# Attention 1: v's blocks filled by transfers in place of copies, operand transfers on two queues

## The chip, the core and the metric

The kernel runs on one core of a Trainium2 chip. The metric is the device time of one execution in microseconds (us), a median over runs. The engines are PE (matrix products; its weight loads are the profile's PEld), DVE (vector), ACT (activations), POOL (GpSimd) and SP, which here only issues transfers (DMAs). Each engine works through its own queue in order and waits for the others by semaphores. DMAs can be issued from SP, POOL or ACT; a DMA that has to wait keeps everything behind it on the issuing queue waiting.

## What is computed

Two layers over x (8 sequences of 1024 tokens, 256 wide): an attention with its residual and normalisation, and a block of a second attention and a mixture of experts. The change concerns only the first attention, in which **every token attends within itself**: its q, k and v are 16 heads of 64 numbers each, and the 64x64 scores are made inside one head of one token.

```python
Q = (x @ Wq + bq).reshape(b, s, H, C) * inv_sqrt_c      # H, C = 16, 64
K = (x @ Wk + bk).reshape(b, s, H, C)
V = (x @ Wv + bv).reshape(b, s, H, C)
scores = jnp.einsum('bshq,bshk->bshqk', Q, K)            # an outer product per token and head
scores = jnp.where(triu_mask, -jnp.inf, scores)
w = jax.nn.softmax(scores, axis=-1)
attn = jnp.einsum('bshqk,bshk->bshq', w, V)
x = layernorm(x + attn.reshape(b, s, H * C) @ Wo + bo)
```

## The kernel before

`phase_a` does this layer; phases B and C do the rest and are not touched. It works through 64 tiles of 128 tokens. A tile `t` is cut into 8 chunks `c`, each of them 64 tokens (`ww = c // 4`, the half of the tile) by four heads (`c % 4`). The main loop writes out by hand, chunk by chunk, what each engine is given; since every engine keeps its order, the order of these calls is the schedule.

**Scores as block matrices.** For PE, an outer product per token and head becomes a matrix product with block-diagonal operands: `R` holds q (and row maxima) on the diagonal blocks, `L` holds k. There are two buffers of each. `build(t, r)` (line 360) fills one pair for the chunks 2r and 2r+1 with 24 DMAs: 8 for `R` (line 370, 16 rows of 2 KB each, issued from POOL) and 16 for `L` (line 376, 64 pieces of 128 B each, issued from SP). A DMA into a buffer waits until the scores of two chunks earlier have read it. `gather(r)` (line 384) puts a small memset, the *event*, on POOL; it waits for all 24 DMAs, and the score matmuls (`scores`, line 418) wait for it alone. ACT takes the exponentials (line 433).

**Sums.** `sums` (lines 453 and 463) multiplies the exponentials with v on PE. Its weights are columns of `V`, one buffer for each half `ww`: 128 partitions, for each head and each of four token groups `u` a block of 32 columns (four tokens times 8, with v in columns 0 to 3 of a token's 8 and a one in column 4, which sums the weights themselves). Four of these matmuls of 32 columns run side by side on quarters of the PE array. The quotients are laid by tokens again: ACT evicts to `S` (line 479), and POOL issues 32 DMAs a tile `nd<-S` (line 489).

**How V is filled.** `proj_v` (line 291) makes v transposed, two halves of 512 columns in PSUM, and DVE evicts each with the bias to `vT` as (channel, chunk of channels, token) at line 306. `spread_v` (line 313) then copies it on DVE into the blocks of V: 8 copies for each half of the tile and each half of the channels, 32 a tile (line 320; 32 partitions, 96 or 128 values each). The calls stand in `fill_a` and `fill_b` at chunks 0 and 6.

**One PSUM buffer `ps`** serves the projections of k, q and v for the next tile, two halves each, at chunks 0 to 5 (`between`), and the output projection at 6 and 7. A projection cannot start before DVE has evicted the one before it; q's evictions are line 331.

**Side work on DVE and POOL.** The rest of the tables `head`, `fill_a`, `middle` and `fill_b` says at which chunk which side job is issued: `divide` (lines 573 to 580: the sums are added up, the reciprocal taken and multiplied) for the tile before, `extrema` (running maxima and minima of k, two scans of DVE), `products` (two multiplications on POOL) and `maxima` (one on DVE) for the next tile, `token_scores`, `token_less`, `token_exp`, `token_sums` for four heads of the present tile that are done without PE, `normal` (line 629) for the normalisation and `store` for the finished rows. An entry's sign says for which tile: "+" the next, "" this, "-" the one before, "--" two before.

**Buffers that matter.** `vT`, `r`, `lo`, `att` have one buffer each, k, qm, x1o and xr two, the pair of score banks three.

Of the kernel before, what the change touches and what calls it, by code (L numbers as in the profile page):

```python
# [165 lines left out]
def phase_a(tc, a, ident, x1_d, norm_scalars, share, view):  # L166
# [19 lines left out]
    with (  # L186
# [68 lines left out]
        for i in range(2):  # L255
            Ls.append(wp.tile([P, 16, 4, 32], FP, name=f"L{i}"))
            R = wp.tile([P, 4, 8, C1], FP, name=f"R{i}") if i else share["R"]
            nc.gpsimd.memset(R, 0.0)
            Rs.append(R)
            V = wp.tile([P, NV, 4, 32], FP, name=f"V{i}") if i else share["V"].rearrange("p j h u c -> p (j h) u c")[:, :NV]  # L260
            nc.gpsimd.memset(V, 0.0)
            for aa in range(4):
                nc.gpsimd.memset(V[32 * aa : 32 * aa + 32, :, :, 8 * aa + 4 : 8 * aa + 5], 1.0)
            Vs.append(V)
# [26 lines left out]
        def proj_v(t, half):  # L291
            if half == 0:
                state["vT", t] = op.tile([P, HID // P, P], FP, name="vT")
            vT = state["vT", t]
            ps = pps.tile([P, 512], FP, name="ps")
            for i in range(4):
                ch = 4 * half + i
                for c in range(DC):
                    nc.tensor.matmul(  # L299
                        ps[:, i * P : (i + 1) * P],  # L300
                        w["v"][:, c, chunk[ch] * P : (chunk[ch] + 1) * P],
                        xT_of[t][:, c, :],
                        start=c == 0,
                        stop=c == DC - 1,
                    )
            nc.vector.tensor_tensor(
                vT[:, 4 * half : 4 * half + 4, :],
                ps.rearrange("p (i t) -> p i t", i=4),
                bv[:, 4 * half : 4 * half + 4, None].to_broadcast([P, 4, P]),
                ALU.add,  # L310
            )

        def spread_v(t, ww, half):

            src = state["vT", t].rearrange("p i (w u a b) -> p i w u a b", w=2, u=4, a=4)
            for qd in (2 * half, 2 * half + 1):
                at, n = (H1, (H1 - HT) // 2) if qd % 2 else (0, H1 // 2)
                V = Vs[ww][:, at : at + 2 * n].rearrange("p (i r) u (a b) -> p i r u a b", r=2, a=4)
                for aa in range(4):
                    nc.vector.tensor_copy(  # L320
                        V[32 * aa : 32 * aa + 32, :, qd // 2, :, aa, 0:4],
                        src[32 * qd : 32 * qd + 32, :n, ww, :, aa, :],
                    )
# [36 lines left out]
        def build(t, r):  # L360
# [7 lines left out]
            for b in range(4):  # L368
                for s in range(2):
                    moved.append((None, nc.gpsimd.dma_start(R[:, b, s, b, :], q[:, b, s, cols])))  # L370
# [65 lines left out]
        def sums(t, c, which):  # L436
# [7 lines left out]
            for x, h in enumerate(heads):  # L444
                hp = h0 + h
                v = 2 * slot[hp // 2] + hp % 2
# [46 lines left out]
        def token_v(t, ps):  # L493

            n = TC // P
            for i in range(n):
                nc.tensor.transpose(ps[:, (2 + i) * P : (3 + i) * P], state["vT", t][:, HID // P - n + i, :], ident)
# [230 lines left out]
        def lead_v(k):  # L728
# [91 lines left out]
        spread_v(0, 0, 0)  # L820
        spread_v(0, 0, 1)
# [9 lines left out]
        for t in range(NT + 1):  # L831
            live, more = t < NT, t + 1 < NT
            for c in range(8):
# [17 lines left out]
                if c == 4 and t > 1:  # L851
# [863 lines left out]
```

## Time and profile before

| | |
|---|---|
| median of 13 runs | 4911.7 us (4898.5 to 4935.2) |
| the profiled execution | 4906.4 us, span in the profile 4904.6 us |
| tiles of phase A | about 62 like ones, 64.5 us apart on the mean (stores at 212.7 to 4144.4 us) |
| busy shares | PE 91%, DVE 85%, ACT 73%, POOL 71% |
| mean granted PE clock | 0.96 |
| DVE copies into V (L320) | 2048, 631.0 us in all |
| DMAs on SP in phase A | L<-k 4088, 0.64 us each to issue |
| DMAs on POOL in phase A | R<-qm 2048 and nd<-S 2048, 0.49 us each |

The profile has one execution. A line such as "PE ps L330 <- DVE qm L331: 244.8, 62, 5.8" in the view of waits says that PE, about to run line 330, stood idle for 244.8 us in all, 62 times, at most 5.8 us, until DVE had done line 331. In the view of groups a line reads: source line, engine, operation, written tile <- read tiles, shapes, count | busy us, mean ns of one | idle before, by releaser. In the timeline a line reads: start us, length us, engine, line, operation, tiles, shapes, count, and in brackets the idle time before it with what ended it. An engine that is busy without a break is not always the bound: what counts is which wait ends last at the place where the time is lost.

### The profile page before, as it was taken

To read this page: it belongs to the slowest core of one execution; us is meant where nothing else is said; L and a number is where in the kernel's file an instruction comes from. 1 tells how busy PE (TensorE), PEld (TensorE's weight loads), DVE (VectorE), ACT (ScalarE), POOL (GpSimd) and SP (SyncE) were. 2 spreads that over 40 slices of the span, in tenths; PEclk is the share of its full clock that TensorE was granted. 3 is DMA by queue.
4 is the path that set the end of the run, shared out by engine and by line. 5 is a ranking of instruction groups with operands and counts; after the bars stand their busy time and mean duration, and the time that the engine had idled before them with its cause. 6 is when DMAs were issued, how large, how long until landed. Compare 5 with 4: busy or idle time off the path is not lost.

```text
span 4904.6 us, 169315 instructions
## 1 busy us (share of the span) xinstructions
PE 4462.2 (91%) x70232; PEld 2998.2 (61%) x70232; DVE 4164.9 (85%) x6686; ACT 3560.9 (73%) x5015; POOL 3471.7 (71%) x5672
## 2 busy tenths in 40 slices
PE   7999999999999999999999999999999999888785
PEld 4666666666666666666666666666666666555564
DVE  7888888888888988898888889888888897577778
ACT  5778777777787887778877877777887788344334
POOL 6777777777777777778777777877777776232346
PEclk9999999999999999999999999999999999999897
DMA  2222212222221222222212222221222222133443
GB/s 80 48 49 50 48 48 50 50 49 48 49 52 46 50 50 49 48 49 52 49 48 51 50 49 48 50 49 47 52 52 48 48 49 71 53 79 77 130 150 117
DMA packets 521271, 285.66 MB, mean 58 GB/s; under 512 B 373425, under 2 KB 439345, under 8 KB 520497
## 3 DMA queue, kind: packets, MB, share of 16 engines
q1 hardware_dynamic: 378466, 113.23, 11.9%
q0 software_dynamic: 139264, 159.69, 10.4%
q8 instruction: 550, 9.01, 0.8%
q10 hardware_dynamic: 2768, 1.91, 0.1%
q14 instruction: 223, 1.83, 0.1%
HBM read 72.84 MB, written 33.85 MB: 22 GB/s over the span
## 4 chain that ended last, share of the span: by engine, by line
PE 60%; DVE 27%; DMA 3%; POOL 3%; issue 2%; ACT 2%; SPq 2%; DVEq 0%; ACTq 0%; POOLq 0%
PE pair L418 16%; PE sum L453 11%; PE sum L463 7%; DVE att L579 5%; PE ps L299 5%; PE ps L618 5%; PE ps L330 4%; PE pair L407 4%; DVE V L320 4%; DVE nd L578 3%; DVE att L580 3%; PE ps L288 2%; SPq L376 2%; PE pair L589 1%; ACT s L1029 1%
## 5 line engine op out<-in xcount | busy, mean ns | idle before, releaser
L433 ACT ACTIVATE e<-pair 128x1024 f32<-128x1024 f32 x2560 | 2481.4, 1022 | 534.1 <-PE pair L418 503.5
L418 PE MATMUL pair<-R,L 32*128 32x128 f32 (+1 forms) x28672 | 1408.7, 321 | 4.8 <-POOL event L384 4.1
L489 POOL DMA_DIRECT2D nd<-S x2048 | 972.6, 483 | 610.6 <-ACT S L479 548.1
L418 PEld LDWEIGHTS pair<-R,L 32*128 32x128 f32 x28672 | 1103.5, 187 | 118.4 <-issue 64.9
L370 POOL DMA_DIRECT2D R<-qm x2048 | 989.6, 490 | 140.6 <-PE pair L418 118.1
L453 PE MATMUL sum<-e,V 128*32 128x256 f32 x12288 | 963.9, 385 | 4.1 <-ACT S L479 4.0
L463 PE MATMUL sum<-e,V 128*32 128x128 f32 x16384 | 792.5, 278 | 0.0
L479 ACT COPY S<-sum 128x512 f32<-128x512 f32 (+1 forms) x1024 | 552.3, 539 | 312.6 <-PE sum L463 312.6
L463 PEld LDWEIGHTS sum<-e,V 128*32 128x32 f32 x16384 | 503.1, 111 | 433.9 <-issue 114.9
L320 DVE COPY V<-vT 32x128 f32<-32x128 f32 (+1 forms) x2048 | 631.0, 308 | 29.3
L330 PE MATMUL ps<-wq,xT 128*128 128x512 f32 x512 | 332.4, 784 | 250.8 <-DVE qm L331 244.8
L544 POOL TENSOR_TENSOR s<-s,qm 128x1024 f32<-128x1024 f32 (+2 forms) x320 | 517.1, 1636 | 3.1
L579 DVE RECIPROCAL att<-nd 128x384 f32<-128x384 f32 (+1 forms) x192 | 438.1, 2282 | 3.9 <-DMA nd<-S 1.7
L407 PE MATMUL pair<-late,sel 32*128 32x256 bf16 (+1 forms) x5120 | 402.1, 299 | 4.2 <-ACT e L433 4.2
L453 PEld LDWEIGHTS sum<-e,V 128*32 128x32 f32 x12288 | 305.4, 109 | 151.4 <-issue 63.4
L76 POOL TENSOR_SCALAR ve<-mv 128x1 f32<-128x1 f32 x128 | 85.0, 664 | 435.1 <-DVE mv L74 417.1
L563 DVE TENSOR_TENSOR s<-s,vt 128x1024 f32<-128x1024 f32 (+2 forms) x320 | 382.0, 1194 | 11.1
L562 DVE TENSOR_REDUCE part<-s 128x64 f32<-128x1024 f32 (+3 forms) x320 | 300.8, 940 | 73.8 <-ACT s L548 73.8
L330 PEld LDWEIGHTS ps<-wq,xT 128*128 128x128 f32 x512 | 108.1, 234 | 384.9 <-DVE qm L331 269.7
L564 DVE TENSOR_REDUCE part<-s 128x64 f32<-128x1024 f32 (+3 forms) x320 | 305.0, 953 | 11.0
L536 DVE TENSOR_TENSOR s<-k,qm 128x1024 f32<-128x1024 f32 (+2 forms) x320 | 292.2, 946 | 0.0
L407 PEld LDWEIGHTS <-sel 32*128 32x128 bf16 x5120 | 135.2, 92 | 242.0 <-issue 234.4
(253 smaller groups left out, 6148.3 us busy)
## 6 DMA issues: line engine op xcount, KB each, us to landing
R<-qm POOLq DMA_DIRECT2D x2048, 32.0 KB, 2.1
nd<-S POOLq DMA_DIRECT2D x2048, 32.0 KB, 2.0
L<-k SPq DMA_DIRECT2D x4088, 8.0 KB
rows_d<-yx SPq DMA_DIRECT2D x32, 512.0 KB
xT<-in_xT SPq DMA_DIRECT2D x64, 128.0 KB
xr<-in_x SPq DMA_DIRECT2D x64, 128.0 KB
x_d<-x1o SPq DMA_DIRECT2D x64, 128.0 KB
w<-in_w SPq DMA_DIRECT2D x32, 256.0 KB
```

The costliest lines, as they stand in the source:

```text
L320: nc.vector.tensor_copy(V[32 * aa : 32 * aa + 32, :, qd // 2, :, aa, 0:4], src[32 * qd : 32 * qd + 32, :n, ww, :, aa, :],)
L330: nc.tensor.matmul(ps, xT_of[t][:, c, :], w["q"][:, c, cols], start=c == 0, stop=c == DC - 1)
L370: moved.append((None, nc.gpsimd.dma_start(R[:, b, s, b, :], q[:, b, s, cols])))
L407: nc.tensor.matmul(bank[u][:, at : at + width].rearrange("p (n i) -> p n i", i=n)[:, :, 0:32], sel[pr].rearrange("p a j -> p (a j)"), late ...
L418: one = nc.tensor.matmul(bank[u][:, x * 4 * n : (x + 1) * 4 * n].rearrange("p (b i) -> p b i", i=n), Lt[pr, 2 * (h0 + h) + jb].rearrange(" ...
L433: nc.scalar.activation(es[i], pair[i], AF.Exp)
L453: nc.tensor.matmul(dst[32 * u : 32 * u + 32], Vs[ww][:, v, u, :], e[u // 2][:, u % 2, x * 256 : (x + 1) * 256].rearrange("p (b i) -> p b i ...
L463: nc.tensor.matmul(dst[32 * u : 32 * u + 32], Vs[ww][:, v if alone else H1 + v, u, :], e2[u // 2][:, u % 2, h * P : (h + 1) * P].rearrange ...
L479: nc.scalar.copy(S[:, :, at : at + 2, i0:].rearrange("p b h i -> p h b i"), ps[:, : 8 * (C1 - i0)].rearrange("p (h b i) -> p h b i", h=2, ...
L489: nc.gpsimd.dma_start(tok[:, b, s, (h0 - G) * C1 : (h0 + G) * C1], Sx[:, 4 if s else b, b, :])
L544: nc.gpsimd.tensor_tensor(s, s, m, ALU.subtract)
L579: nc.vector.reciprocal(att[:, cols], nd[:, 1, cols])
```

## The change

Four things are changed together.

- **V is filled by DMA.** `V` is kept as four quarters (`blocks`, by halves of a channel chunk and of the kind of head), each laid out as 32 columns `m`, then channel chunks `i`, then token groups `u`. A block column's values for all `i` and `u` are thus neighbours (128 or 96 B), and `spread_v` is 16 DMAs from SP for each half of the tile, each 32 partitions by 4 such rows. So that the source has the same layout, `proj_v` reads x in the order (w, m, u) instead of token order, and the eviction writes `vT` as (m, i, u). The block for the four token-wise heads is evicted a second time in token order, `vo`, by two operations on DVE. `sums` reads its weights from the quarters, 32 columns in steps of n x 4 values (n is 8 or 6).
- **Operand transfers:** all of R is issued from SP; of the 16 DMAs for L the odd `u` go from POOL, the even from SP. In the first tile the L that ACT issued now go from POOL too.
- **Order:** the second `products` moves from chunk 5 to the head of chunk 7 (ahead of the event there), the second `extrema` from 4 to 5, the second `maxima` from 6 to 7, the last `divide` from 1 to 2, `normal` from the first half of chunk 2 to the end of chunk 4, `store` from 4 to 6. The two calls of `spread_v` for each half become one, at chunks 0 and 6 in `fill_a`.
- x1o has one buffer instead of two.

```diff
+            V = wp.tile([P, NV * P], FP, name=f"V{i}") if i else share["V"].rearrange("p j h u c -> p (j h u c)")[:, : NV * P]
             nc.gpsimd.memset(V, 0.0)
+            blocks, at = [], 0
+            for qd in range(4):
+                n = (H1 - HT * (qd % 2)) // 2
+                blocks.append(V[:, at : at + n * P].rearrange("p (m i u) -> p m i u", m=32, u=4))
+                at += n * P
+                for aa in range(4):
+                    nc.gpsimd.memset(blocks[qd][32 * aa : 32 * aa + 32, 8 * aa + 4 : 8 * aa + 5], 1.0)
+            Vs.append(blocks)
...
                     nc.tensor.matmul(
-                        ps[:, i * P : (i + 1) * P],
+                        ps[:, i * P : (i + 1) * P].rearrange("p (w m u) -> p w m u", w=2, u=4),
                         w["v"][:, c, chunk[ch] * P : (chunk[ch] + 1) * P],
-                        xT_of[t][:, c, :],
+                        xT_of[t][:, c, :].rearrange("p (w u m) -> p w m u", w=2, u=4),
...
             nc.vector.tensor_tensor(
-                vT[:, 4 * half : 4 * half + 4, :],
-                ps.rearrange("p (i t) -> p i t", i=4),
-                bv[:, 4 * half : 4 * half + 4, None].to_broadcast([P, 4, P]),
+                vT[:, :, 4 * half : 4 * half + 4, :].rearrange("p m i u -> p i m u"),
+                ps.rearrange("p (i m u) -> p i m u", i=4, u=4),
+                bv[:, 4 * half : 4 * half + 4, None, None].to_broadcast([P, 4, 32, 4]),
                 ALU.add,
             )
+            if half == 1:
+                for i in range(TC // P):
+                    nc.vector.tensor_scalar(
+                        state["vo", t][:, i, :].rearrange("p (w u m) -> p w u m", w=2, u=4),
+                        ps[:, (2 + i) * P : (3 + i) * P].rearrange("p (w m u) -> p w u m", w=2, u=4),
+                        bv[:, 6 + i : 7 + i], None, ALU.add,
+                    )
...
-        def spread_v(t, ww, half):
+        def spread_v(t, ww):
+            src = state["vT", t].rearrange("p (w a b) i u -> p w a b i u", w=2, a=4)
+            for qd in range(4):
+                V = Vs[ww][qd].rearrange("p (a b) i u -> p a b i u", a=4)
+                n = V.shape[3]
                 for aa in range(4):
-                    nc.vector.tensor_copy(
-                        V[32 * aa : 32 * aa + 32, :, qd // 2, :, aa, 0:4],
-                        src[32 * qd : 32 * qd + 32, :n, ww, :, aa, :],
+                    nc.sync.dma_start(
+                        V[32 * aa : 32 * aa + 32, aa, 0:4].rearrange("p b i u -> p b (i u)"),
+                        src[32 * qd : 32 * qd + 32, ww, aa, :, :n, :].rearrange("p b i u -> p b (i u)"),
                     )
...
-                    moved.append((None, nc.gpsimd.dma_start(R[:, b, s, b, :], q[:, b, s, cols])))
+                    moved.append((None, nc.sync.dma_start(R[:, b, s, b, :], q[:, b, s, cols])))
...
-                    queue = nc.scalar if t + r == 0 and aa % 2 else nc.sync
+                    queue = nc.gpsimd if u % 2 else nc.sync
...
-                            Vs[ww][:, v, u, :],
+                            v[0][:, :, i, u],
...
-                        Vs[ww][:, v if alone else H1 + v, u, :],
+                        v[0 if alone else 1][:, :, i, u],
...
-            o = xp.tile([P, D], FP, name="x1o")
+            o = op.tile([P, D], FP, name="x1o")
...
         head = {
...
+            7: [("+", products, 1)],
         fill_a = {
-            0: [("", spread_v, 1, 0)],
-            2: [("--", normal), ("-", residual)],
+            0: [("", spread_v, 1)],
+            2: [("-", residual)],
             3: [("+", products, 0)],
-            5: [("+", products, 1), ("-", residual_bias)],
-            6: [("+", spread_v, 0, 0)],
+            5: [("-", residual_bias)],
+            6: [("+", spread_v, 0)],
...
         fill_b = {
-            0: [("", spread_v, 1, 1), ("+", extrema, 0)],
-            1: [("-", divide, 1), ("", token_scores, "F"), ("-", divide, 2)],
-            2: [("", token_sums, "A")],
+            0: [("+", extrema, 0)],
+            1: [("-", divide, 1), ("", token_scores, "F")],
+            2: [("-", divide, 2), ("", token_sums, "A")],
             3: [("", token_sums, "B"), ("", token_scores, "C")],
-            4: [("+", maxima, 0), ("+", extrema, 1), ("", token_sums, "F"), ("-", turn)],
-            6: [("+", spread_v, 0, 1), ("+", maxima, 1)],
-            7: [("+", token_scores, "A"), ("+", token_scores, "B"), ("", divide, 0)],
+            4: [("+", maxima, 0), ("--", normal), ("", token_sums, "F"), ("-", turn)],
+            5: [("+", extrema, 1)],
+            7: [("+", maxima, 1), ("+", token_scores, "A"), ("+", token_scores, "B"), ("", divide, 0)],
...
-                if c == 4 and t > 1:
+                if c == 6 and t > 1:
                     store(t - 2)
```

More of the change, by code (lines that the diff above doesn't have):

```diff
@@ L259, in phase_a @@
             Rs.append(R)
-            V = wp.tile([P, NV, 4, 32], FP, name=f"V{i}") if i else share["V"].rearrange("p j h u c -> p (j h) u c")[:, :NV]
+            V = wp.tile([P, NV * P], FP, name=f"V{i}") if i else share["V"].rearrange("p j h u c -> p (j h u c)")[:, : NV * P]
             nc.gpsimd.memset(V, 0.0)
-            for aa in range(4):
-                nc.gpsimd.memset(V[32 * aa : 32 * aa + 32, :, :, 8 * aa + 4 : 8 * aa + 5], 1.0)
-            Vs.append(V)
+            blocks, at = [], 0
[6 more added lines that the diff above has]
+            Vs.append(blocks)
         def preset(i):
@@ L292, in proj_v @@
             if half == 0:
-                state["vT", t] = op.tile([P, HID // P, P], FP, name="vT")
+                state["vT", t] = op.tile([P, 32, HID // P, 4], FP, name="vT")
+                state["vo", t] = op.tile([P, TC // P, P], FP, name="vo")
             vT = state["vT", t]
@@ L306, in proj_v @@
             nc.vector.tensor_tensor(
-                vT[:, 4 * half : 4 * half + 4, :],
-                ps.rearrange("p (i t) -> p i t", i=4),
-                bv[:, 4 * half : 4 * half + 4, None].to_broadcast([P, 4, P]),
+                vT[:, :, 4 * half : 4 * half + 4, :].rearrange("p m i u -> p i m u"),
+                ps.rearrange("p (i m u) -> p i m u", i=4, u=4),
+                bv[:, 4 * half : 4 * half + 4, None, None].to_broadcast([P, 4, 32, 4]),
                 ALU.add,
             )
-        def spread_v(t, ww, half):
[L315 to L318, printed above, removed]
+            if half == 1:
[3 more added lines that the diff above has]
+                        ps[:, (2 + i) * P : (3 + i) * P].rearrange("p (w m u) -> p w u m", w=2, u=4),
+                        bv[:, 6 + i : 7 + i],
+                        None,
+                        ALU.add,
+                    )
[4 more added lines that the diff above has]
+                n = V.shape[3]
                 for aa in range(4):
-                    nc.vector.tensor_copy(
-                        V[32 * aa : 32 * aa + 32, :, qd // 2, :, aa, 0:4],
-                        src[32 * qd : 32 * qd + 32, :n, ww, :, aa, :],
+                    nc.sync.dma_start(
+                        V[32 * aa : 32 * aa + 32, aa, 0:4].rearrange("p b i u -> p b (i u)"),
+                        src[32 * qd : 32 * qd + 32, ww, aa, :, :n, :].rearrange("p b i u -> p b (i u)"),
                     )
@@ L445, in sums @@
                 hp = h0 + h
-                v = 2 * slot[hp // 2] + hp % 2
+                v = Vs[ww][2 * (hp % 2) : 2 * (hp % 2) + 2]
+                i = slot[hp // 2]
                 if alone:
@@ L496, in token_v @@
             for i in range(n):
-                nc.tensor.transpose(ps[:, (2 + i) * P : (3 + i) * P], state["vT", t][:, HID // P - n + i, :], ident)
+                nc.tensor.transpose(ps[:, (2 + i) * P : (3 + i) * P], state["vo", t][:, i, :], ident)
             state["vt", t] = xp.tile([P, TC], FP, name="vt")
@@ L819, in phase_a @@
         proj_v(0, 1)
-        spread_v(0, 0, 0)
-        spread_v(0, 0, 1)
+        spread_v(0, 0)
         token_v(0, pps.tile([P, 512], FP, name="ps"))
```

## The prediction

> **What bounds the kernel now.** I read the page's busy shares first, then the waits of PE, then single tiles in the timeline and in the windows view, and last the chain. A tile is 128 tokens; the stores of the finished rows (x_d<-x1o, one a tile) lie 64.5 us apart on the mean from 212.7 us to 4144.4 us, so about 62 such tiles make four fifths of the span and everything that the diff touches.
>
> ```profile
> PE 4462.2 (91%) x70232; PEld 2998.2 (61%) x70232; DVE 4164.9 (85%) x6686; ACT 3560.9 (73%) x5015; POOL 3471.7 (71%) x5672
> ```
> ```profile
> PE ps L330 <- DVE qm L331: 244.8, 62, 5.8
> ```
>
> PE is the busiest, and the only long wait of PE in a tile is one: the second half of the q projection (L330) waits until DVE has evicted the first half (L331), because both use the one PSUM buffer `ps`. It happens in every tile. The windows view of a common tile and of a rare one (60.5 us) shows what it costs; columns are length, busy time of PE, PEld, DVE, ACT, POOL, then the granted clock:
>
> ```profile
> 1511.60:1577.10 65.50, 60.44 (x1040) 39.73 (x1040) 56.77 (x83) 49.70 (x63) 48.71 (x83) 0.95 0.20 48
> 406.90:467.40 60.50, 59.05 (x1054) 39.91 (x1050) 52.06 (x86) 50.91 (x65) 48.49 (x83) 1.00 0.22 52
> ```
>
> The common tile has 5.06 us of idle PE and a clock of 0.95; the short one has 1.45 us and a full clock. So PE's own work is 59.05 us a tile, and the common tile pays twice: for the wait, and for slower matmuls after it. The timeline shows both, first on DVE, then on PE:
>
> ```profile
> 1533.75 6.66 DVE L320 COPY V<-vT 32x128 f32<-32x128 f32 x8
> ...
> 1549.93 2.54 DVE L579 RECIPROCAL att<-nd 128x384 f32<-128x384 f32 x1
> 1552.50 1.90 DVE L580 TENSOR_TENSOR att<-att,nd 128x384 f32<-128x384 f32 x1
> 1554.33 1.22 DVE L629 TENSOR_SCALAR x1o<-r,mv,rs 128x256 f32<-128x256 f32 x1
> 1555.47 0.68 DVE L331 SCALAR_TENSOR_TENSOR qm<-ps,bias 128x512 f32<-128x512 f32 x1
> ```
> ```profile
> 1544.84 1.99 PE L330 MATMUL ps<-wq,xT 128*128 128x512 f32 x4
> ...
> 1556.20 3.78 PE L330 MATMUL ps<-wq,xT 128*128 128x512 f32 x4 [5.06 <-DVE qm L331]
> ```
>
> The first projection ends at 1546.8, but DVE is solidly busy from 1532 and reaches its eviction only at 1555.5; after the wait the same four matmuls take 3.78 us for 1.99 (the windows view grants a clock of 0.50 there).
>
> **Part 1: what goes.** The copies of L320 go (32 a tile, 631.0 us in all, 9.9 us a tile). In the stretch before the eviction of q that is 1.8 + 6.66 us; the last division (2.54 + 1.90) and the normalisation x1o (1.22) move behind it, to chunks 2 and 4. DVE would reach L331 some 14 us earlier, where 1555.5 - 1546.8 = 8.7 us are enough. So the wait goes whole, and DVE falls from 56.8 to about 47 us a tile. Behind the next eviction of q stand the last division and the sums of A (4.4 + 3.7 us), a chunk is over 7 us: late by at most 1 us, and the next user of `ps` comes a chunk later. Gain 64.5 - 59.05 = **5.4 us a tile**, 338 us over 62; nothing in the trace speaks for more. It is covered by nothing else: PE is the chain there.
>
> **Part 2: PE reads in steps.** The v projection now reads x by tokens 16 columns (64 B) apart, and the sums load V weights in steps of 96 or 128 B. No matmul or weight load of this trace reads fp32 in such steps, so I bound it. Below: no cost, because the sums run four at a time, four streams side by side: eight L453 of 256 columns take 0.46 us, 0.23 for each round of four, where a single stream (L618, 256 columns, 1.73 us for 8) takes 0.22; the reading side isn't short. Above: the two nearest rows, reductions of DVE over 512 values, one with values 256 B apart, the other packed:
>
> ```profile
> L1388 DVE TENSOR_REDUCE loc<-run 128x64 f32<-128x512 f32 x1 | 1.0, 1012 | 0.0
> L1424 DVE TENSOR_REDUCE total<-run 128x64 f32<-128x512 f32 x1 | 0.7, 686 | 0.0
> ```
>
> The steps cost 326 ns over 512 values, 0.64 ns each. For the projection: 32 matmuls a tile of 128 columns, 82 ns each, now one every 0.111 us (2.05 us for 16): **+2.6 us a tile**, straight on PE. I take this end: it is the only row with the pattern. For the weights: 32 columns, 20 ns, behind a round of matmuls (0.108 us or more) except the first of the 16 groups: **+0.3 us**. If instead the four loads of a round share one way, 128 columns cost 82 ns in each of the 64 rounds of L463, whose matmuls leave no room: +5.2 us, the upper bound.
>
> This row can be weighed against a rule. The Trainium skill, page "Advanced Engine Details and Errata", section "Memory Cachelines", says that SBUF is read at full rate only where at least two accesses fall on one 16-byte line; here every value lies on a line of its own, so it speaks against this change. DVE's row agrees in kind (1.5 times), no run here shows PE. Taken as half rate for PE, an estimate from the page, the projection would cost 3.4 us a tile in place of 2.6 and the sum would be some 50 us higher.
>
> **Part 3: queues.** POOL gives its 32 transfers R to SP and takes 32 of the 64 L. An L has 64 pieces of 128 B where R has 16. What POOL takes for 64 is not in the trace; the nearest rows are 16 rows and, with an index, 128 rows:
>
> ```profile
> L370 POOL DMA_DIRECT2D R<-qm x2048 | 989.6, 490 | 140.6 <-PE pair L418 118.1 <-issue 10.0 <-DVE nd L578 5.1
> ...
> L1505 POOL DMA_INDIRECT g<-rows_d,token x64 | 61.6, 962 | 57.6 <-ACT w L1362 38.4 <-issue 18.0 <-PE ps L1519 1.2
> ```
>
> Between 0.49 and 0.96 us; a straight line by pieces gives 0.69, which I take: +0.2 x 32 = 6.4 us a tile, POOL 48.7 to 55 of 60. POOL matters through one instruction, the event that lets PE use the new operands (L384). Its tightest place is the chunk pair 0 and 1:
>
> ```profile
> 1528.08 3.89 POOL L370 DMA_DIRECT2D R<-qm  x8
> 1531.97 3.80 POOL L489 DMA_DIRECT2D nd<-S  x8
> 1535.79 3.83 POOL L544 TENSOR_TENSOR s<-s,qm 128x1024 f32<-128x1024 f32 x2
> 1539.56 0.09 POOL L384 MEMSET event<- 1x1 f32 x1
> ```
>
> PE asked for it at 1541.1, 1.5 us later. The eight L add 1.6 us, and the second products (3.3 us) now stand in chunk 7 ahead of the event and the root of the norm, where POOL idled 2.2 us: everything after starts 1.1 us later. 1.6 + 1.1 - 1.5 = **+1.2 us a tile** (0 at 0.49 us an L; 3.4 at 0.96). Waiting behind it are only the next L and nd. The page "DMA: Bandwidth & Descriptors" of the Trainium skill ("Anatomy of one DMA") holds that many descriptors are emitted before their cost shows; by that this term is 0.
>
> SP issued 64 L of 0.69 us (11.08 for 16) and now issues 32 L, 32 R, 32 V. R and V cost 0.34 to 0.64; the nearest is lg_d<-bias, 128 pieces, 0.43. In all 22 + 28 + 1.3 = 51 us of about 63. In chunks 6 and 0 the V come behind the operands: 8 x 0.43 + 8 x 0.69 = 9 us for operands (11 before), then 7 us for V, 16 of the 14 to 17 us that a pair of chunks lasts; V is first read 6.7 us into chunk 0 for one half and in chunk 4 for the other. I put it at 0, hidden under the scores; at 0.64 each the next operands start 4 us late and about 2 us reach PE. R behind the last maxima (now chunk 7) waits about as long as the event, already counted. DVE's two extra evictions `vo` (about 0.3 us each) and the eviction by blocks lie in DVE's new slack. The single buffer for x1o: its next write is a tile after the store, 0. The first tile pays once: R and V now queue on SP behind the last maxima, about +5 us.
>
> **Sum.** A tile: -5.4 + 2.6 + 0.3 + 1.2 = -1.3 us; x 62 = -81, + 5 = -76. The profiled execution took 4906.4 us (span 4904.6), the median of the runs is 4911.7, 0.1% above it; against the median: **4835 us**.
>
> **Rivals.**
> - *PE doesn't mind the steps.* For it: four streams at full rate. Against it: the DVE row. -5.4 + 1.2 = -4.2 a tile, 4655 us; with L at 0.49 as well 4580.
> - *Weight loads become the bound (slower).* Place: the 64 rounds of L463 a tile, whose loads (0.110 us) are already as long as their matmuls (0.108). Price +5.2 for +0.3: 3.6 us a tile, +225, 5140 us. It decides from 20 ns more a round (64 x 0.020 = 1.3). Against it: the loads of a round start 7 ns apart and end together.
> - *POOL becomes the bound.* At 0.96 us an L its busy time is 48.7 + 15 = 64 us, with its waits for ACT (1 to 3 us a tile) 66 to 67, above the 64.5 of today: +2 x 62, about 5040 us. For it: 64 pieces, not 16.
> - *The change doesn't do what it says:* PE still waits at L330. Only if DVE is held by another wait; then PE stalls as now and pays for the steps: about 5070.
>
> **Chances.** Forecast (4750 to 4915) 0.36; steps free 0.27; weight loads 0.16; POOL 0.12; L330 or a late SP queue 0.09. The forecast's own spread crosses zero: of its 0.36, 0.28 are faster by over 0.2% (about what a measurement of this kernel can tell from no change) and 0.04 each within and slower. With the others: faster 0.57 (0.28 + 0.27 + 0.02), same 0.05, slower 0.38. The range 4620 to 5090 leaves out the lowest corner of the free steps and the upper half of the weight loads, less than 2 in 10.
>
> **What would show it.** Right: the wait of L330 gone, clock 1.00 in every tile, L320's group gone from DVE; L299's 16 matmuls at about 3.3 us for 2.05 (free: still 2.05); L463's weight loads near 0.13 us and its eight matmuls still 0.22 us apart (rival: 0.30); L on POOL at 0.69; PE waiting about 1 us a tile for the event. Wrong at once: a tile above 64.5 us, whichever engine is solid in it.

## The result, and the profile after

The changed kernel takes **5678.1 us** (median of 8 runs, 5669.9 to 5684.5) where the kernel before takes 4911.7 (37 runs): ratio 1.156, 95% interval 1.154 to 1.158. It is 766 us slower; the forecast was 77 us faster, and 5678 lies far outside the range.

Two lines of the page after, the busy shares and the chain that ended last, and one of the waits of PE (us in total, times, longest):

```profile
PE 4904.8 (87%) x70232; PEld 3514.3 (62%) x70232; DVE 3590.4 (63%) x4766; ACT 3584.5 (63%) x5015; POOL 3628.4 (64%) x5696
PE 40%; SPq 37%; DVE 8%; DMA 6%; issue 5%; ACT 3%; POOL 1%; POOLq 0%; ACTq 0%; DVEq 0%
```
```profile
PE pair L433 <- POOL event L399: 561.8, 128, 9.0
```

No engine is as full as PE was before, and VectorE lost 574.5 us of busy time (4164.9 to 3590.4), 9.0 us a tile, near the 9.8 of the forecast (56.8 to 47); its share fell further, from 85 to 63 percent, because the span grew. But SPq, the queue that only issues DMAs, stands on 37 percent of the chain. The 244.8 us of waiting at the q projection are gone; in their place the scores wait 562 us, twice in a tile, for the event that says that their operands have landed. The chain points at the queue; the busy shares could not, since what SP does to issue a DMA is not counted as busy there.

A tile, here the median distance between two stores x_d<-x1o of a trace (64 in each), grew from 65.2 to 75.7 us. Over the 63 distances that is 709.5 us (mean 63.27 to 74.53), the first store comes 51.8 us later (its place in the program is two chunks further on, and the tiles before it are slow too; how the 51.8 us divide was not measured), and what follows the last store is 2.7 us shorter: together the 758.6 us by which the span grew.

The timeline of SP in the tile after, from the operands for the next tile (built in chunk 6) on; start, duration, line, transfer, count:

```profile
2003.13 4.98 SPq L385 DMA_DIRECT2D R<-qm  x8
2008.16 5.55 SPq L391 DMA_DIRECT2D L<-k  x8
...
2014.81 12.09 SPq L335 DMA_DIRECT2D V<-vT  x16
2027.00 4.99 SPq L385 DMA_DIRECT2D R<-qm  x8
2032.03 5.54 SPq L391 DMA_DIRECT2D L<-k  x8
2037.68 11.28 SPq L335 DMA_DIRECT2D V<-vT  x16
2049.06 5.66 SPq L385 DMA_DIRECT2D R<-qm  x8
2054.76 5.54 SPq L391 DMA_DIRECT2D L<-k  x8
```

SP has no gap from 2003 to 2071. The second group of operands stands behind V of the first window, the third behind both groups of V. PE in the same stretch, with its two waits and a v projection; then the windows view of the work behind the first wait, of the second wait, of the work behind that, and of the whole tile (length; busy PE, PEld, DVE, ACT, POOL; then the granted clock, the share of its full clock that PE was given):

```profile
2039.43 1.24 PE L433 MATMUL pair<-R,L 32*128 32x128 f32 x16 [3.19 <-POOL event L399]
...
2062.16 2.09 PE L433 MATMUL pair<-R,L 32*128 32x128 f32 x32 [5.57 <-POOL event L399]
...
2067.92 3.72 PE L305 MATMUL ps<-xT,wv 128*128 128x128 f32 x16
```
```profile
2039.40:2043.60 4.20, 4.17 (x68) 3.29 (x68) 4.10 (x8) 1.84 (x2) 3.66 (x6) 0.60 0.26 31
2056.60:2062.10 5.50, 0.00 (x0) 0.00 (x0) 2.87 (x3) 0.62 (x2) 0.09 (x2) 0.80 0.16 33
2062.10:2067.00 4.90, 4.84 (x72) 3.48 (x76) 0.00 (x0) 1.98 (x3) 4.90 (x7) 0.53 0.25 61
```
```profile
2014.31:2090.55 76.24, 67.49 (x1062) 48.89 (x1058) 50.29 (x55) 51.44 (x65) 52.32 (x83) 0.93 0.24 48
```

The third group's last L is issued at 2060.3, the event runs at 2062.0, PE follows at 2062.2. The tile has 76.24 - 67.49 = 8.75 us of idle PE, which is just these two waits (3.19 + 5.57). Behind each, the clock is at 0.60 and 0.53, so the busy time itself holds slow matmuls; the first experiment shows how many.

### The profile page after: what moved, and what is told of

It is laid out like the page before. It is cut to its first block, busy times and chain, and to the rows that moved or that the text cites. A ratio compares the mean times of both kernels' runs of the same rounds, so it can differ in the third digit from the quotient of the medians.

```text
span 5663.2 us, 170670 instructions
## 1 busy us (share of the span) xinstructions
PE 4904.8 (87%) x70232; PEld 3514.3 (62%) x70232; DVE 3590.4 (63%) x4766; ACT 3584.5 (63%) x5015; POOL 3628.4 (64%) x5696
## 4 chain that ended last, share of the span: by engine, by line
PE 40%; SPq 37%; DVE 8%; DMA 6%; issue 5%; ACT 3%; POOL 1%; POOLq 0%; ACTq 0%; DVEq 0%
SPq L335 13%; SPq L385 12%; SPq L391 12%; PE pair L433 12%; PE ps L305 7%; PE sum L469 7%; PE sum L479 4%; DMA L<-k 3%; PE pair L422 2%; PE ps L345 2%; DMA V<-vT 1%; ACT s L1045 1%; DVE part L578 1%; PE pair L605 1%; PE ps L634 1%
## 5 line engine op out<-in xcount | busy, mean ns | idle before, releaser
L433 PE MATMUL pair<-R,L 32*128 32x128 f32 (+1 forms) x28672 | 1521.6, 340 | 562.7 <-POOL event L399 561.8
L433 PEld LDWEIGHTS pair<-R,L 32*128 32x128 f32 x28672 | 1190.3, 204 | 713.8 <-POOL event L399 633.5
L391 POOL DMA_DIRECT2D L<-k x2048 | 1281.9, 632 | 222.7 <-PE pair L433 179.2
L469 PE MATMUL sum<-e,V 128*32 128x256 f32 x12288 | 1110.9, 434 | 5.3 <-ACT S L495 4.0
L479 PEld LDWEIGHTS sum<-e,V 128*32 128x32 f32 x16384 | 655.0, 152 | 329.0 <-issue 136.7
L479 PE MATMUL sum<-e,V 128*32 128x128 f32 x16384 | 856.7, 292 | 1.7 <-DMA V<-vT 1.7
L312 DVE TENSOR_TENSOR vT<-ps,bv 128x512 f32<-128x512 f32 x128 | 88.5, 692 | 913.2 <-PE ps L305 909.4
L469 PEld LDWEIGHTS sum<-e,V 128*32 128x32 f32 x12288 | 452.7, 175 | 166.2 <-issue 75.6
L305 PE MATMUL ps<-xT,wv 128*128 128x128 f32 x2048 | 479.0, 401 | 1.6 <-DVE qm L346 0.8
L305 PEld LDWEIGHTS ps<-xT,wv 128*128 128x128 f32 x2048 | 409.6, 205 | 63.0 <-issue 23.2
L359 DVE TENSOR_TENSOR_SCAN lo<-lim_lo,k 128x512 f32<-128x512 f32 x128 | 335.7, 2623 | 0.0
```

The source lines that it names most:

```text
L305: nc.tensor.matmul(ps[:, i * P : (i + 1) * P].rearrange("p (w m u) -> p w m u", w=2, u=4), w["v"][:, c, chunk[ch] * P : (chunk[ch] + 1) * ...
L391: one = queue.dma_start(Lt[u, aa, :, 0, :, aa, :], k[u, aa, :, 16 * g : 16 * g + 16, :])
L433: one = nc.tensor.matmul(bank[u][:, x * 4 * n : (x + 1) * 4 * n].rearrange("p (b i) -> p b i", i=n), Lt[pr, 2 * (h0 + h) + jb].rearrange(" ...
L469: nc.tensor.matmul(dst[32 * u : 32 * u + 32], v[0][:, :, i, u], e[u // 2][:, u % 2, x * 256 : (x + 1) * 256].rearrange("p (b i) -> p b i", ...
L479: nc.tensor.matmul(dst[32 * u : 32 * u + 32], v[0 if alone else 1][:, :, i, u], e2[u // 2][:, u % 2, h * P : (h + 1) * P].rearrange("p (b ...
```

## The experiments

The theory: SP's issue queue is too long where the operands are due. Rivals: the stepped reads on TensorE alone; POOL with its heavier L; the landing of the transfers, not their issue. Ratios are to the kernel before on the same chip; beside the first four experiments that took 4965 us, beside the others 4913 and 4914. So where one of the first four is set against another kernel, the times carry about a percent of difference between chips, and the ratio is the safer figure.

**V's transfers left out after the first tile** (`v_left_out`, against the kernel after):

```diff
         def spread_v(t, ww):
+            if t > 0:
+                return
```

> The 32 transfers of V in a tile are left out after the first tile (the sums go on with the first tile's values of v), everything else is as after the change, the stepped reads of TensorE included. Theory (SP's queue): in a tile SP loses 23.4 of its 68 us (two groups of 16, 12.1 and 11.3 us), the operands R and L come in time, the waits of the scores for the event (3.2 and 5.6 us a tile) and the slow clock behind them go. What is left is 59.05 of PE's own work + 3.4 (v projection) + 0.8 (weight loads) + about 1 (event on POOL) = 64.3 us a tile for 76.2: about 4940 us. Rival "the steps on PE alone": they are all still there, so 5600 to 5680. Rival "POOL": its 32 L, its products and the event's place are unchanged, so 5600 to 5680.

Measured: 4890.1 us, ratio to before 0.985 (0.982 to 0.989). The wait for the event, and a common tile in the windows view:

```profile
PE pair L434 <- POOL event L400: 12.1, 4, 6.1
```
```profile
2010.00:2073.30 63.30, 63.30 (x1054) 46.41 (x1054) 45.32 (x55) 51.15 (x64) 52.93 (x83) 1.00 0.26 51
```

The waits go from 128 to 4, the clock is 1.00, PE is solid. So 32 transfers on SP cost the median tile 12.4 us (75.7 to 63.3). In the tile shown above, of 76.24 us, it is 12.94: 8.75 of waits, and 67.49 - 63.30 = 4.19 of slow matmuls behind them. POOL, its L and its event are as after: as a cause it is out.

**V by copies, all else as after** (`v_copied`): the DMA in `spread_v` becomes VectorE's `tensor_copy` into the new blocks, in halves:

```diff
-                    nc.sync.dma_start(
+                    nc.vector.tensor_copy(
                         V[32 * aa : 32 * aa + 32, aa, 0:4].rearrange("p b i u -> p b (i u)"),
...
-            0: [("", spread_v, 1)],
+            0: [("", spread_v, 1, 0)],
...
-            6: [("+", spread_v, 0)],
+            6: [("+", spread_v, 0, 0)],
...
-            0: [("+", extrema, 0)],
+            0: [("", spread_v, 1, 1), ("+", extrema, 0)],
...
+            6: [("+", spread_v, 0, 1)],
```

> V is filled by copies of VectorE again, in halves and in the places where they stood before, but into the new layout by blocks, so that the projection, the sums, the queues of R and L and the order of the divisions are as after the change. Theory (SP's queue): as without the transfers, 64.3 us a tile and about 4940 us, at most 60 more if the copies (about 10 us a tile of a VectorE that is busy for 63 percent of 76 us) delay an eviction. Rivals "steps alone" and "POOL": 5600 to 5680, since PE's reads and POOL's work are unchanged.

Measured: 5087.5 us, ratio 1.025 (1.022 to 1.028), tile 66.5. The waits for the event are gone here too, but I was 90 to 150 us low. The waits view shows what came, and the timeline of VectorE and POOL why:

```profile
PE ps L305 <- DVE qm L346: 171.5, 63, 3.4
```
```profile
2048.87 2.04 DVE L335 COPY V<-vT 32x128 f32<-32x128 f32 x8
...
2051.66 5.97 DVE L335 COPY V<-vT 32x128 f32<-32x128 f32 x8
```
```profile
2049.16 3.87 POOL L505 DMA_DIRECT2D nd<-S  x8
2053.05 3.85 POOL L560 TENSOR_TENSOR s<-s,qm 128x1024 f32<-128x1024 f32 x2
```

Eight such copies take 2.04 us beside POOL's DMA issues and 5.97 beside POOL's arithmetic. In the trace it is one of the eight that is held, for 4.36 us, until about 0.1 us after the arithmetic ends; of the 2048 copies of the run the 66 that meet POOL's arithmetic take 4.4 us on the mean, the others 0.2. So VectorE, with the copies, is late for the second half of q, and the v projection waits for it 2.7 us a tile.

**The projection packed** (`x_packed`):

```diff
-  ps[:, i * P : (i + 1) * P].rearrange("p (w m u) -> p w m u", w=2, u=4),
+  ps[:, i * P : (i + 1) * P],
...
-  xT_of[t][:, c, :].rearrange("p (w u m) -> p w m u", w=2, u=4),
+  xT_of[t][:, c, :],
...
-                ps.rearrange("p (i m u) -> p i m u", i=4, u=4),
+                    ps.rearrange("p (i w u m) -> p w i m u", i=4, w=2, u=4)[:, w_],
```

> The v projection reads x packed, and its eviction does the reordering from PSUM (in two instructions for one); everything else is as after the change. Theory (SP's queue): the 16 matmuls of a group take 2.05 us again for 3.7 (3.4 us a tile), but SP's 68 us and its order are unchanged, so PE waits longer for the event instead: 5600 to 5680 us. Rival "the steps on PE set the time": 3.4 x 62 = 211 us less, 5470 us or below.

Measured: 5621.8 us, ratio 1.133 (1.129 to 1.137), tile 74.7. PE in the timeline:

```profile
2025.25 2.09 PE L434 MATMUL pair<-R,L 32*128 32x128 f32 x32 [6.66 <-POOL event L400]
2030.51 2.05 PE L305 MATMUL ps<-xT,wv 128*128 128x128 f32 x16
```

The projection takes 2.05 us again for 3.72, about 3.4 us a tile. PE gives most of it back as a longer wait (6.66 for 5.57; over the run 657.5 us for 561.8): the tile is 1.0 us shorter. A saving on an engine that waits for something else is worth little.

**V of the second window one pair of chunks later** (`v_later`):

```diff
-            0: [("", spread_v, 1)],
-            2: [("-", residual)],
+            2: [("", spread_v, 1), ("-", residual)],
```

> The transfers of V for the second window are issued a pair of chunks later: behind the operands of chunks 4 and 5 instead of in front of them. SP has the same 68 us of work in a tile, in another order. Theory (SP's queue, its order as much as its sum): the operands of chunks 4 and 5 come some 11 us sooner, so PE's wait for them (5.6 us) and the slow clock behind it go; the wait of chunk 2 (3.2 us, behind the V of the first window) stays; V itself may be 0 to 2 us late at chunk 4. 3 to 7 us a tile gained, 5250 to 5500 us. If only SP's sum counted: 5650 to 5690. Rivals "steps alone" and "POOL": no change, 5660 to 5690.

Measured: 5289.7 us, ratio 1.066 (1.063 to 1.070), tile 69.5. The same transfers in another order are worth 388 us by the times (1.156 to 1.066 by the ratios); one wait remains:

```profile
PE pair L433 <- POOL event L399: 288.6, 72, 6.0
```

The 69.5 us that are left are nearly SP's own 68 us of issue.

**Both repairs** (`packed_v_left_out`: the diffs of `x_packed` and `v_left_out` together).

> Both repairs together: V's transfers left out after the first tile (the sums go on with the first tile's v) and the v projection reads x packed. Theory (the stepped read costs 3.4 us a tile, but only where SP's queue doesn't set the end): the tile falls from 63.3 (V left out alone) to about 59.9, PE's own work plus the weight loads, and the time from 4890 by 3.4 x 62 = 211 to about 4680 (4640 to 4720). Rival (the steps are hidden behind something else, as a packed read beside the queue gained only 1 percent): no lower than 4850.

Measured: 4633.3 us, ratio 0.943 (0.942 to 0.945). A common tile:

```profile
2026.20:2086.14 59.94, 59.94 (x1058) 43.82 (x1054) 46.20 (x57) 51.05 (x65) 52.16 (x83) 1.00 0.27 53
```

Here the packed read is worth 63.30 - 59.94 = 3.36 us a tile, over three times the 1.0 us by which it shortened the tile behind the queue. And 59.94 - 59.05 = 0.9 us is what is left for the weight loads of V in steps. The windows view of these matmuls alone says the same: first the v projection in a tile of `v_left_out` and in this one, then the tile `sum` in this one and in a tile of `order_alone` (below), where V's weights lie packed; the second number is PE's busy time, and the clock is full in all four:

```profile
2010.00:2073.30 63.30, 7.52 (x32) 6.41 (x32) 1.00 0.26 51
2026.20:2086.14 59.94, 4.10 (x32) 3.72 (x32) 1.00 0.27 53
2026.20:2086.14 59.94, 21.60 (x448) 16.11 (x448) 8.64 (x17) 1.00 0.27 53
2000.00:2061.00 61.00, 20.67 (x448) 12.25 (x448) 8.63 (x16) 1.00 0.21 52
```

That is 3.42 us for the projection and 0.93 for the sums.

**A quarter of each transfer** (`v_quarter`):

```diff
-  V[32 * aa : 32 * aa + 32, aa, 0:4].rearrange("p b i u -> p b (i u)"),
-  src[32 * qd : 32 * qd + 32, ww, aa, :, :n, :].rearrange("p b i u -> p b (i u)"),
+  V[32 * aa : 32 * aa + 32, aa, 0].rearrange("p i u -> p (i u)"),
+  src[32 * qd : 32 * qd + 32, ww, aa, 0, :n, :].rearrange("p i u -> p (i u)"),
```

> Each of the 32 transfers of V moves a quarter of its pieces (32 of 128, one block row of four; the rest of V stays as set at the start, so the sums lack three quarters of v). Nothing else differs. Rival A (SP's issue of a transfer has a fixed price): the group of 16 still takes 11 to 12 us on SP and the kernel 5640 to 5690. Rival B (the price goes by the pieces, or by the bytes landed, since a transfer waits for the one eight before it): a group takes about 16 x 0.42 = 7 us, as for xT and xr, SP has 8 to 10 us less in a tile, and the kernel takes 5150 to 5350.

Measured: 5624.3 us, ratio 1.145 (1.143 to 1.147). SP's two groups of V in one tile:

```profile
2006.20 11.88 SPq L335 DMA_DIRECT2D V<-vT  x16
...
2028.87 11.01 SPq L335 DMA_DIRECT2D V<-vT  x16
```

A quarter of the bytes and of the pieces costs SP the same 11 to 12 us. The price is that of a transfer, not of its data. Nor is it a wait for earlier transfers to land (in the trace's records a transfer also waits for the one eight before it): in `v_left_out` the eight R behind a pause of 6.1 us on SP take 5.77 us:

```profile
2010.04 0.41 SPq L600 DMA_DIRECT2D x_d<-x1o  x1
2016.55 5.77 SPq L386 DMA_DIRECT2D R<-qm  x8
```

So the landing of V's data is out as a cause too.

**The order alone** (`order_alone`, against the kernel before):

```diff
-            2: [("--", normal), ("-", residual)],
+            2: [("-", residual)],
...
-            1: [("-", divide, 1), ("", token_scores, "F"), ("-", divide, 2)],
-            2: [("", token_sums, "A")],
+            1: [("-", divide, 1), ("", token_scores, "F")],
+            2: [("-", divide, 2), ("", token_sums, "A")],
...
-            4: [("+", maxima, 0), ("+", extrema, 1), ("", token_sums, "F"), ("-", turn)],
+            4: [("+", maxima, 0), ("+", extrema, 1), ("--", normal), ("", token_sums, "F"), ("-", turn)],
...
-                if c == 4 and t > 1:
+                if c == 6 and t > 1:
...
-            o = xp.tile([P, D], FP, name="x1o")
+            o = op.tile([P, D], FP, name="x1o")
```

> The kernel before with one part of the change alone: the last division in chunk 2, the normalisation x1o in chunk 4 with its own buffer and the store in chunk 6; V by copies, its layout, the projection and the queues as before. Theory (the wait at the q projection comes from what stands ahead on VectorE): 5.66 us less stand there, the wait (5.06 us) and the slow clock go for the most part, 64.5 to about 60 us a tile, 4640 (4600 to 4720), ratio about 0.94. Rival (the work moved behind delays the next eviction, as with the copies in the new layout, where the v projection waited 2.7 us a tile for the second half of q): 62 to 63 us a tile, 4760 to 4830, ratio 0.97 to 0.985.

Measured: **4690.8 us, ratio 0.954 (0.953 to 0.956)**, tile 61.0. The part that only moves three things, and gives x1o one buffer, takes 4.6 percent off by itself. The 5.06 us wait at the q projection is gone; of the rival's kind a remnant is there:

```profile
PE ps L299 <- DVE qm L331: 68.4, 51, 2.6
```

**The queues alone** (`queues_alone`, against the kernel before):

```diff
-  moved.append((None, nc.gpsimd.dma_start(R[:, b, s, b, :], q[:, b, s, cols])))
+  moved.append((None, nc.sync.dma_start(R[:, b, s, b, :], q[:, b, s, cols])))
...
-                    queue = nc.scalar if t + r == 0 and aa % 2 else nc.sync
+                    queue = nc.gpsimd if u % 2 else nc.sync
```

> The kernel before with the queues of the operands alone changed: R on SP, every second L on POOL; V by copies, order and projection as before. SP has 32 x 0.65 + 32 x 0.69 + 1.3 = 44 us a tile for 45, so SP can't be late; POOL has 32 x (0.63 - 0.49) = 4.5 us more. Theory: the wait at the q projection still sets the tile, 4890 to 4970 us (ratio 0.99 to 1.01). Rival (POOL's heavier transfers delay the event): 1 to 2 us a tile more, ratio 1.015 to 1.025.

Measured: 4973.9 us, ratio 1.012 (1.010 to 1.014), between the two ranges. Neither mechanism is right: PE waits at the q projection more than before (301.8 us for 244.8, 57 of the 61 us), not for the event. Among the groups of VectorE one stands out, the scan `lo`, here and before:

```profile
L344 DVE TENSOR_TENSOR_SCAN lo<-lim_lo,k 128x512 f32<-128x512 f32 x128 | 496.8, 3881 | 0.0
L344 DVE TENSOR_TENSOR_SCAN lo<-lim_lo,k 128x512 f32<-128x512 f32 x128 | 249.4, 1949 | 0.0
```

It is held by POOL, whose work now falls on other moments: 122 of the 128 scans overlap POOL's arithmetic, 64 before; those that do not take 1.2 us in both.

**x1o to ScalarE** (`order_x1o_act`, against `order_alone`):

```diff
-            nc.vector.tensor_scalar(o, r, mean, rs, ALU.subtract, ALU.mult)
+            nm = xp.tile([P, 1], FP, name="nm")
+            nc.gpsimd.tensor_scalar(nm, mean, rs, -1.0, ALU.mult, ALU.mult)
+            nc.scalar.activation(o, r, AF.Identity, bias=nm, scale=rs)
```

> The order part alone (last division in chunk 2, x1o in chunk 4, store in chunk 6), and the normalisation x1o taken from VectorE to ScalarE (one activation with scale and bias; the bias, a product of 128 values, is one more small instruction on POOL). In the run of the order part alone x1o took 5.41 us in a common tile where 0.82 is its time when POOL is idle; its 1.75 us on the mean leave VectorE. Theory (VectorE, held up while POOL computes, is what keeps that kernel 1.9 us a tile above PE's own 59.05): 1 to 2 us a tile less, 4560 to 4640 for 4690. Rival (the hold-up only moves to the next instruction on VectorE, because POOL's work is the same): 4660 to 4700.

Measured: 4676.0 us, ratio 0.952 (0.950 to 0.954): not told apart from `order_alone`. My theory falls. VectorE lost 78 us of busy time (4261.6 to 4183.8) and the kernel some 15. x1o did not stand in front of the larger wait for VectorE, which stays at 68.1 us; a smaller one (35.8 us at L497) goes, but some 20 us of new waits for ScalarE, which now has x1o, come in its place. What binds there is PE, as a tile of `order_alone` shows:

```profile
2000.00:2061.00 61.00, 59.07 (x1051) 39.95 (x1050) 58.90 (x84) 50.73 (x65) 48.26 (x83) 1.00 0.21 52
```

PE is busy 59.07 of 61.0 us at full clock. At most 1.9 us a tile are left to win without less work for PE.

**Half of V by DMA** (`v_half_by_dma`: `x_packed`, with V of the second window by copies of VectorE at chunk 0, in the places of `v_copied`).

> After the change, with the v projection packed and V of the second window filled by copies of VectorE in two halves; V of the first window still comes by 16 transfers on SP. SP has 68 - 11.3 = 57 us of work in a tile. Theory (it is SP's sum against PE's 60 us, and the order): the sum fits now, and only the place behind V, the operands of chunks 2 and 3, can be late: 10.6 + 11.7 + 10.6 = 33 us of issue from chunk 6 on for two pairs of chunks of 15 us, so a wait of 1 to 3 us a tile for the event; 61 to 63 us, 4700 to 4820. If a single transfer of V too many were enough to spoil it (the price lies in the transfers themselves, not in SP's sum): above 5000.

Measured: 5120.4 us, ratio 1.042 (1.040 to 1.045), tile 67.9: 300 us above the upper end of what I expected, and in the range set for the other reading (above 5000). SP, the event, and PE's wait for it in the whole run:

```profile
2003.44 11.24 SPq L336 DMA_DIRECT2D V<-vT  x16
2014.78 4.99 SPq L386 DMA_DIRECT2D R<-qm  x8
2019.82 5.54 SPq L392 DMA_DIRECT2D L<-k  x8
```
```profile
2026.93 0.09 POOL L400 MEMSET event<- 1x1 f32 x1 [5.31 <-DMA L<-k]
```
```profile
PE pair L434 <- POOL event L400: 332.1, 65, 7.9
```

The place was right: the operands of chunks 2 and 3, behind V. The wait is 332.1 us over 65 times, 5.1 us for my 1 to 3: I left out the 1.6 us from the last issue (2025.4) to the event. And I priced the wait without the slow clock behind it (the run's mean clock is 0.945, that of `packed_v_left_out` 0.981). SP has 57 us of issue in 67.9 and stands idle in parts of the tile, yet it is still what PE waits for: the place of the transfers in the queue decides, not the sum.

**Half of V on ScalarE's queue** (`v_on_act`, `x_packed` with one more edit):

```diff
-                    nc.sync.dma_start(
+                    (nc.scalar if ww else nc.sync).dma_start(
```

> After the change, with the v projection packed and the 16 transfers of V for the second window issued by ScalarE's queue instead of SP's; those of the first window stay on SP. Same transfers, same bytes. Theory (the price is the issuing engine's time, about 0.65 us a transfer wherever it is paid): SP has 57 us, ScalarE 50 + 10.4 = 60 to 61 us of a tile, in one piece of 10 us at chunk 0 in which no exponential runs; PE, with three buffers of scores, runs out of work for 6 to 9 us: 66 to 69 us a tile, 5010 to 5200. Rival (an issue is only dear on SP because its queue is full; ScalarE hands transfers over in 0.1 to 0.2 us): 61 to 63 us a tile, 4700 to 4820.

Measured: 5827.8 us, ratio 1.186 (1.183 to 1.189), tile 78.9, the slowest of all and above both ranges. ScalarE, and PE's wait for it:

```profile
2008.97 0.59 ACT L496 COPY S<-sum 128x512 f32<-128x512 f32 x1
2015.21 11.74 ACTq L336 DMA_DIRECT2D V<-vT  x16
2027.06 1.94 ACT L449 ACTIVATE e<-pair 128x1024 f32<-128x1024 f32 x2 [17.49 <-DMA V<-vT]
```
```profile
PE pair L423 <- ACT e L449: 1075.0, 69, 19.6
```

The price is the same there, 11.74 us for 16; the 0.1 to 0.2 us of the rival stand in no trace of this case, where no issue on SP or ScalarE takes less than 0.27. I had left out a wait in front of it. In the records of this trace the transfers of both queues take turns on the same eight completion counters, and each waits for the last transfer on its counter. So ScalarE does nothing from 2009.6 to 2015.2: its first V waits for a transfer that SP issues only at 2013.0 (the third of the R that start at 2011.7). All exponentials stand behind it, 17.5 us in a tile, and PE waits 15.6 us for them.

## Why the prediction was wrong

**The step that failed** is "I put it at 0, hidden under the scores", SP's queue in part 3. Two things were wrong in it.

*The size.* R and V were put at 0.43 us, by lg_d<-bias, a transfer to DRAM, with 0.64 as the worst. They took 0.62 to 0.71 (R, 4.98 to 5.66 for 8) and 0.70 to 0.76 (V, 11.28 and 12.09 for 16). The text had the nearer row one sentence before: L, from one tile in SBUF to another and on the same queue, 0.69. I chose the row by its number of pieces, and `v_quarter` shows that pieces are not what is paid for. SP had 68 us to issue in a tile, not 51. With the 0.69 of L for all three kinds the same sum would have read 96 x 0.69 + 1.3 = 67.5 us, more than the 63 it was set against.

*The working.* Even 0.64 was said to make the operands 4 us late. I set each pair of chunks against its own transfers, and the sum of the tile against 63 us; but a queue carries its backlog on. From chunk 6 to the operands of chunks 4 and 5 it has to issue three groups of R and L and both groups of V, 2003.1 to 2060.3, 57 us; at PE's own pace (63.3 us for eight chunks) those three pairs of chunks last 47. That the sum of a tile fits says little. In `v_half_by_dma` it does, and PE still waits 5.1 us a tile; in `v_later` it is the same 68 us as after, in another order, and the kernel is 388 us faster (9 percent of the kernel before, by the ratios).

*The price of the wait.* Of the 12.94 us in the tile shown, 4.19 are no wait but matmuls at a clock of 0.5 to 0.6 behind one. I had counted this double price as a gain at the q projection and did not count it as a loss here; a late SP queue got, together with the wait at L330, 0.09 of the chances and no time of its own among the rivals.

The other steps, each with what it measured:

- *The wait at the q projection, -5.4:* right. It is gone from the trace after, and `order_alone` has 61.0 us a tile. PE's own 59.05 was right as well: 59.07 in that tile. But the gain needs only the order: with V still filled by copies, all but 1.9 us a tile of it is there.
- *The projection in steps, +2.6:* 3.36, when PE sets the time. After, L305's 16 matmuls take 3.72 us for 2.05, 1.8 times. The row of VectorE gave 1.5 times; the half rate that I had taken, as an estimate, from the rule in the Trainium skill ("Advanced Engine Details and Errata", section "Memory Cachelines") gave 3.4 and was the better guide. PE's trace agrees with that rule in kind: where every value lies on a line of its own, the read is slower.
- *Weight loads, +0.3:* about 0.9 (59.94 - 59.05; 0.93 in the sums alone). The loads of L479 take 152 ns for 111 on the mean, so they do get longer, but the rival with 5.2 us a tile was far off. (In the trace before, the loads of a round start 7 ns apart and also end some 7 ns apart, not together, as I had read them.)
- *POOL, +1.2:* about 0. L took 0.63 us there for my 0.69, against 0.49 for R, so 64 pieces do take POOL longer than 16, and the reading by which this term is 0 is not what the trace shows. But the event had room for it: in `v_left_out` PE waits for it 4 times in the whole run. Tried without the rest, the queues cost something else, VectorE held by POOL (`queues_alone`, 61 us), which I did not have.
- *The sum* with these sizes and without SP is 59.05 + 3.42 + 0.93 = 63.4 us, with the two prices taken from the matmuls themselves; `v_left_out` shows 63.3. One term, at 0 for 12.4 us a tile, made nearly the whole error; most of the rest lies ahead of the first store, 51.8 us late for my 5. The ratio of `v_left_out`, 0.985, is close to the 0.984 of the forecast, but that is in part luck: the two step terms were 1.4 us a tile too low together, and POOL's was 1.2 too high.

## What to carry to other kernels

Treat every queue that issues DMAs as an engine with a fixed price per transfer, taken from the nearest row of the same kind (from where to where, on which queue), and lay its list out against the times at which its results are due, with the backlog carried from stage to stage. Before trading copies on one engine for many small transfers, count the transfers, not their bytes, and look what stands behind them in that queue. And try the parts of a change one by one: here the part that cost nothing, moving three steps to later chunks, by itself takes the kernel to 4691 us from 4913.

## What the runs showed of the hardware

- A transfer from SBUF to SBUF costs the issuing engine 0.62 to 0.77 us on SP and 0.73 on ScalarE's queue (groups of 8 and 16, gaps included), alike for 8 KB in 64 pieces, 32 KB in 16 and a quarter of either V. Issued from POOL it took 0.49 us for 16 pieces and 0.63 for 64. The Trainium skill, page "DMA: Bandwidth & Descriptors", section "Issuing engines are not separate DMA queues", calls the time to initiate a DMA usually small beside the DMA itself. Here it is not: an issue takes 0.7 us beside 1.6 us from the last issue to the event (`v_half_by_dma`), and in the kernel after the issues are 68 us of a 76 us tile. The measurement decides.
- VectorE is held while POOL computes: a copy of 0.2 us takes 4.4 us where it meets POOL's arithmetic, and ends about 0.1 us after it (`v_copied`). The Trainium skill, page "SBUF — State Buffer", section "Who interferes with whom", has the rule: a copy in a mode that uses both of VectorE's ports shares a pair of ports with GpSimd, and whoever comes second is blocked for the whole instruction; an operation with two SBUF inputs contends with GpSimd's reads. The traces agree in kind; in which mode the copies ran no run here shows. Which instruction it hits moves with every change of order (the scan `lo`: 1949 ns before, 3881 in `queues_alone`, 1395 in `order_alone`), so VectorE's mean times of one kernel are no prices for the next.
- A matmul that reads fp32 in steps of 64 B runs at little over half its rate (3.72 us for 2.05 in 16 matmuls of 128 columns).
- A wait of 3.2 us on PE is followed by 4.2 us of work at a granted clock of 0.60, one of 5.6 us by 4.9 us at 0.53: in this kernel 8.75 us of waiting cost 4.19 us more in slower matmuls.
